# Softmax denominators by 32x32 turns and sums on VectorE, with their inverses spread by way of DRAM

## The chip, the cores and the metric

The kernel runs on one core of a Trainium2 chip. The metric is device time in microseconds (us) of one execution. The core's engines are named as in the profile: PE is TensorE (PEld its weight loads), DVE is VectorE, ACT is ScalarE, POOL is GpSimd, and SP is the engine whose queue issues nearly all DMAs.

## The reference

One transformer block with windowless attention and relative positions, followed by a Fourier layer. Only the attention matters here. All data are float32.

```python
B, H, W, C = 1, 48, 48, 768            # 2304 tokens, 12 heads of 64
xn = layernorm(x, ln1_g, ln1_b)
q, k, v = xn @ qkv_w + qkv_b           # each (12, 2304, 64)
attn = einsum('bqc,bkc->bqk', q * 64**-0.5, k)
attn = attn + rel_h[:, :, :, :, None] + rel_w[:, :, :, None, :]
attn = softmax(attn, axis=-1)
out = einsum('bqk,bkc->bqc', attn, v)  # divided by the softmax's denominators
x = x + out @ proj_w + proj_b
x = x + mlp(layernorm(x))              # GELU, 4 * 768 wide
x = x + spectral_layer(x)              # FFT, two complex block-diagonal layers, inverse FFT
```

## The kernel before

The program goes through normalisation with q, k and v (to about 420 us of the profiled execution), attention (to about 1460), the output projection, the MLP with row transforms, and the spectral layer. The change lies in attention.

Attention is cut into 36 blocks: six head pairs `pr` of two heads each, and in each pair six groups `c` of G = 384 queries. Scores are kept transposed, with 128 keys on partitions and queries along the free dimension, so a softmax denominator is a sum over partitions. A block runs in two phases on TensorE:

- Scores. For each of NT = 18 key tiles `kt`, `content` (L560) multiplies keys by queries and `position` (L569) adds the two relative terms by way of a selection matrix, both into a PSUM tile `sp` with three buffers. ScalarE takes the exponential of each (L579) into `exps`. No maximum is subtracted. VectorE adds the exponentials up two key tiles at a time (`pairs`, L659, eight sums per block) and folds the result into `acc` (L663), a tile of 128 partitions by 2 heads by 384 queries. Only the sum over the partitions is then left.
- Products. In six steps of three key tiles, `products` (L592) multiplies values by exponentials into the PSUM tile `op`. Between the steps, small jobs from the table `between` are put in: `relative` (L292) prepares the row terms of a block three ahead, `columns` (L268) the column terms of the next pair. Both write a PSUM bank `small` (there is one), which ScalarE copies twice (L236, L237) and VectorE splits into two parts (`row_lo`, `col_lo`, L238). After `relative`, SP issues 24 DMAs that repeat the row and column terms into `terms` (L305, L309).

Before step 5, `denominators` multiplies `acc` by a matrix of ones (L603), which sums over the partitions and leaves each head's denominators on all of its 64 partitions. ScalarE copies them to `rden` and also sums them into `sums` (L608). After the last step, `finish` copies `op` to `ot` (L617, ScalarE), adds the value bias times the denominator (L618, VectorE), inverts the denominators (L621), multiplies (L623), adds the inverses into `inverse` (L624, GpSimd) and writes the result to DRAM (`oT`, L625, SP). In the blocks c = 2 and 3, `in_columns` (L584) then copies three slices each of the next pair's queries into `by_column` on ScalarE.

`sums` and `inverse` serve a test after attention: if a denominator or an inverse is not below 1e15, an attention with subtracted maxima runs instead. With the given inputs it doesn't.

The order of the work is fixed in two ways. These lines put the queues of TensorE, SP and ScalarE into the order in which the program states their instructions:

```python
with tc.manual_schedule(engines={mybir.EngineType.PE, mybir.EngineType.SP}):
    ...
                with tc.manual_schedule(engines={mybir.EngineType.Activation}):
```

For VectorE and GpSimd a scheduler chooses the order when the program is laid out, from when it expects operands to be ready and, among ready instructions, by their place in the program. [...]

Of the kernel before, what the change touches and what calls it, by code (L numbers as in the profile page):

```python
# [10 lines left out]
F32 = mybir.dt.float32  # L11
# [3 lines left out]
ALU = mybir.AluOpType  # L15
# [31 lines left out]
def block_then_afno(  # L47
# [42 lines left out]
    def col(i):  # L90
        return vec[:, i : i + 1]
# [9 lines left out]
    k_d = [dram.tile([P, T], F32, name=f"k_d{i}") for i in range(NC)]  # L101
    v_d = dram.tile([T, C], F32, name="v_d")
    oT = dram.tile([C, T], F32, name="oT")

    big1 = ctx.enter_context(tc.tile_pool(name="big1", bufs=1))
    main = big1.tile([P, NT * C], F32, name="main")
# [84 lines left out]

    with ExitStack() as flag_scope:
        flag_pool = flag_scope.enter_context(tc.tile_pool(name="flag", bufs=1))
        sums = flag_pool.tile([P, NC * (T // G)], F32, name="sums")
        inverse = flag_pool.tile([P, G], F32, name="inverse")
        nc.vector.memset(inverse, 0.0)


# [5 lines left out]
        with ExitStack() as att:  # L204
# [18 lines left out]
            def small_bank():  # L223
                banks.append(banks.pop(0))
                return banks[-1]
# [317 lines left out]
            with tc.manual_schedule(engines={mybir.EngineType.PE, mybir.EngineType.SP}):  # L543
                with ExitStack() as qkv:
                    queries_keys_values(qkv)

                psum = att.enter_context(tc.tile_pool(name="ps_att", bufs=1, space=PSUM))
                small_banks(psum, 1)
                kv_b = att.enter_context(tc.tile_pool(name="att_kv_b", bufs=1))
                o_pool = att.enter_context(tc.tile_pool(name="att_o", bufs=2))  # L550

                by_column = o_pool.tile([P, HW, HW], F32, name="by_column", bufs=1)
                kv = [None, kv_b]
                exps = main.rearrange("p (n j q) -> p n j q", n=NT, j=2)

                def content(pr, c, kt, sp, first):
                    qT, kT = heads[pr][:2]
                    for j in range(2):
                        at = slice(64 * j, 64 * j + 64)
                        nc.tensor.matmul(  # L560
                            sp[:, j, :G], kT[at, ts(kt, P)], qT[at, ts(c, G)],
                            start=first, stop=not first,
                        )

                def position(pr, c, kt, sp, first):
                    a, b = divmod(kt, 3)
                    for j in range(2):
                        at = slice(64 * j, 64 * j + 64)
                        nc.tensor.matmul(  # L569
                            sp[:, j, :G], select[at, a % 2], ready[pr, c][at, a // 2, b],  # L570
                            start=first, stop=not first,
                        )

                def scores(pr, c, kt, p):

                    sp = psum.tile([P, 2, 512], F32, name="sp", bufs=3)
                    for n, part in enumerate((content, position)):
                        part(pr, c, kt, sp, n == 0)
                    nc.scalar.activation(p, sp[:, :, :G], AF.Exp, scale=HD**-0.5)  # L579

                def in_columns(pr, i):

                    q = heads[pr][0].rearrange("p (c b h w) -> p b w c h", c=6, b=3, h=8)
                    nc.scalar.copy(  # L584
                        by_column[:, ts(i, 8)].rearrange("p w (c h) -> p w c h", c=6),
                        q[:, i // 2, ds(8 * (i % 2), 8)],
                    )

                def products(op, v, kts):
                    for kt in kts:  # L590
                        for j in range(2):
                            nc.tensor.matmul(  # L592
                                op[ts(j, 64)], v[:, kt, ts(j, 64)], exps[:, kt, j, :],
                                start=(kt == 0), stop=(kt == NT - 1),
                            )

                made = {}

                def denominators(pr, c, acc):

                    den = small_bank()
                    for j in range(2):
                        nc.tensor.matmul(  # L603
                            den[ts(j, 64)], ones[:, 0:64], acc[:, j, :], start=True, stop=True
                        )
                    at = pr * (T // G) + c
                    rden = o_pool.tile([P, G], F32, name="rden", bufs=1)
                    nc.scalar.activation(  # L608
                        rden, den, AF.Identity, accum_out=sums[:, at : at + 1]
                    )  # L610
                    made[pr, c] = rden

                def finish(pr, c, op):

                    rden = made.pop((pr, c))
                    ot = o_pool.tile([P, G], F32, name="ot")
                    nc.scalar.copy(ot, op)  # L617
                    nc.vector.scalar_tensor_tensor(  # L618
                        ot, rden, col(V_VB + pr), ot, ALU.mult, ALU.add
                    )  # L620
                    nc.vector.reciprocal(rden, rden)  # L621
                    o = o_pool.tile([P, G], F32, name="o")
                    nc.vector.tensor_tensor(by_rows(o), by_blocks(ot), by_blocks(rden), ALU.mult)  # L623
                    nc.gpsimd.tensor_tensor(inverse, inverse, rden, ALU.add)  # L624
                    nc.sync.dma_start(out=oT[ts(pr, P), ts(c, G)], in_=o)  # L625

                def between(pr, c, acc):

                    last = pr == NC - 1
                    work = {5: [partial(denominators, pr, c, acc)]}  # L630
                    if c < 3:
                        work[0] = [partial(relative, pr, c + 3)]
                    elif not last and c < 5:
                        for n in range(3):
                            work[n] = [partial(columns, pr + 1, 3 * (c - 3) + n)]
                        if c == 4:
                            work[3] = [partial(relative, pr + 1, 0)]
                    elif not last:
                        work[0] = [partial(relative, pr + 1, 1)]
                        work[2] = [partial(relative, pr + 1, 2)]  # L640
                    return work

                with tc.manual_schedule(engines={mybir.EngineType.Activation}):
                    for pr in range(NC):
                        for c in range(T // G):
                            if c == 1 and pr < NC - 1:
                                fetch(pr + 1, kv[(pr + 1) % 2])
                            if c == 2 and pr < NC - 1:
                                fetch_values(pr + 1)
                            if c == 4 and pr == NC - 1:  # L650
                                nc.sync.dma_start(
                                    out=pw, in_=proj_w.rearrange("(c p) f -> p c f", p=P)
                                )
                            pairs = o_pool.tile([P, 2, 2, G], F32, name="pairs", bufs=1)
                            for kt in range(NT):
                                scores(pr, c, kt, exps[:, kt])
                                if kt > 2 and kt % 2:
                                    so_far = exps[:, ds(0, 2)] if kt == 3 else pairs
                                    nc.vector.tensor_tensor(  # L659
                                        pairs, so_far, exps[:, ds(kt - 1, 2)], ALU.add  # L660
                                    )
                            acc = o_pool.tile([P, 2, G], F32, name="acc")
                            nc.vector.tensor_tensor(acc, pairs[:, 0], pairs[:, 1], ALU.add)  # L663
                            op = psum.tile([P, G], F32, name="op")
                            work = between(pr, c, acc)
                            for i in range(6):
                                for what in work.get(i, ()):
                                    what()
                                products(op, heads[pr][2], range(3 * i, 3 * i + 3))
                            finish(pr, c, op)  # L670
                            if c in (2, 3) and pr < NC - 1:
                                for i in range(3):
                                    in_columns(pr + 1, 3 * (c - 2) + i)

        ln2 = flag_scope.enter_context(tc.tile_pool(name="ln2", bufs=4))
        for i in range(4):
# [847 lines left out]
```

## Time and profile before

| | us |
|---|---|
| median of 3 runs (lowest to highest) | 2895.36 (2893.09 to 2896.4) |
| the profiled execution's own time | 2893.09 |
| span of its profile | 2891.3 |
| PE busy in the span | 2833.2 (98%) |
| DVE busy | 1754.9 (61%) |
| ACT busy | 932.2 (32%) |
| POOL busy | 616.9 (21%) |

The granted clock of TensorE was 0.998 over the span. A busy time counts a group's instructions from start to modelled end with overlaps merged; two TensorE instructions that overlap in the array are each listed with their whole duration. A float32 matmul appears as two instructions. "Idle before, releaser" names the instruction whose end ended the idle time. The profile's times run from the span's start.

### The profile page before, as it was taken

Reading aid. Unit: us, or ns where it says so; the run is one execution under the profiler, and the core shown is the slowest. Engines: PE = TensorE matmul, PEld = TensorE weight load, DVE = VectorE, ACT = ScalarE, POOL = GpSimd, SP = SyncE. Lnnn points to the kernel's source line nnn. Section 1 sums busy time; section 2 is a strip of 40 time slices with the busy share of each in tenths; the row PEclk is TensorE's granted clock in tenths of the full one; section 3 lists DMA queues with packets and bytes.
Section 4 is the critical chain, followed back from the end, with each engine's and each line's share of the span. In section 5 each row is a group of like instructions: output and inputs, shape, how many; then the busy total and the mean of one; then the engine's idle time right before and its main releaser. Section 6 shows DMA issues by size and latency. Waiting matters only on the chain. (4 is left out here: it accounts for less than half of the span.)

```text
span 2891.3 us, 41229 instructions
## 1 busy us (share of the span) xinstructions
PE 2833.2 (98%) x15949; PEld 1724.3 (60%) x15949; DVE 1754.9 (61%) x2412; ACT 932.2 (32%) x1538; POOL 616.9 (21%) x589
## 2 busy tenths in 40 slices
PE   8999999999999999999999999999999999999998
PEld 5555655655555555555555555555555555556887
DVE  5243236767676776767633666675666666666666
ACT  1011125757566665665500210112110211012332
POOL 2303010000000000000043223333323322321433
PEclk9999999999999999999999999999999999999999
DMA  4323276262552716435252111212211211113254
GB/s 153 130 96 107 104 161 127 37 130 58 87 125 42 145 31 107 105 59 87 59 178 77 50 53 57 66 44 88 66 55 55 99 55 55 55 56 114 63 158 143
DMA packets 216572, 255.59 MB, mean 88 GB/s; under 512 B 22220, under 2 KB 197036, under 8 KB 214832
## 3 DMA queue, kind: packets, MB, share of 16 engines
q1 hardware_dynamic: 213928, 251.03, 34.1%
q8 instruction: 128, 2.10, 0.3%
q10 hardware_dynamic: 2440, 1.84, 0.2%
q14 instruction: 76, 0.62, 0.1%
HBM read 136.88 MB, written 52.20 MB: 65 GB/s over the span
## 5 line engine op out<-in xcount | busy, mean ns | idle before, releaser
L579 ACT ACTIVATE main<-sp 128x768 f32<-128x768 f32 x648 | 512.6, 811 | 28.2 <-PE sp L569 14.0
L659 DVE TENSOR_TENSOR pairs<-pairs,main 128x1536 f32<-128x1536 f32 x252 | 443.1, 1758 | 27.1 <-DVE pairs L659 0.9
L569 PE MATMUL sp<-terms,select 64*128 64x384 f32 x1296 | 412.3, 629 | 0.0
L1057 DVE TENSOR_TENSOR main<-o,main 128x384 f32<-128x384 f32 x540 | 299.3, 556 | 39.6 <-PE o L1055 1.3
L995 PE MATMUL h<-shared,w 128*128 128x384 f32 x864 | 296.6, 486 | 0.8 <-issue 0.8
L560 PE MATMUL sp<-shared 64*128 64x384 f32 x1296 | 265.9, 486 | 8.0 <-ACT main L579 5.9
L560 PE MATMUL sp<-qT,kT 64*128 64x384 f32 x1296 | 264.4, 485 | 3.5 <-ACT main L579 3.5
L624 POOL TENSOR_TENSOR inverse<-inverse,rden 128x384 f32<-128x384 f32 x36 | 49.0, 1361 | 989.7 <-DVE rden L621 940.3
L449 PE MATMUL m<-main 128*128 128x384 f32 x756 | 246.0, 487 | 3.3 <-DVE main L176 2.7
L995 PEld LDWEIGHTS h<-shared,w 128*128 128x128 f32 x864 | 164.1, 190 | 116.6 <-issue 3.2
L995 PE MATMUL h<-shared,w1s 128*128 128x384 f32 x648 | 226.6, 486 | 0.0
L592 PE MATMUL op<-main,shared 128*64 128x384 f32 x1296 | 218.7, 487 | 0.0
L592 PE MATMUL op<-main,v 128*64 128x384 f32 x1296 | 217.7, 487 | 0.0
L1001 ACT ACTIVATE hT<-c,vec 128x384 f32<-128x384 f32 x108 | 66.4, 615 | 465.9 <-DVE c L1007 465.8
L449 PEld LDWEIGHTS m<-main 128*128 128x128 f32 x756 | 142.9, 190 | 104.0 <-issue 4.8
L1007 DVE TENSOR_TENSOR c<-h,u 128x384 f32<-128x384 f32 x108 | 60.2, 557 | 212.3 <-PE h L995 212.3
L1055 PE MATMUL o<-w,hT 128*128 128x384 f32 x432 | 175.5, 488 | 3.1 <-DVE mv L122 2.0
L1055 PE MATMUL o<-w2s,hs 128*128 128x384 f32 x432 | 175.0, 487 | 3.0 <-DVE hs L159 3.0
L569 PEld LDWEIGHTS sp<-terms,select 64*128 64x128 f32 x1296 | 125.4, 186 | 83.6
L995 PEld LDWEIGHTS h<-shared,w1s 128*128 128x128 f32 x648 | 123.1, 190 | 85.9
L618 DVE SCALAR_TENSOR_TENSOR ot<-rden,vec,ot 128x384 f32<-128x384 f32 x36 | 23.8, 660 | 244.2 <-ACT ot L617 244.2
L158 POOL TENSOR_TENSOR w1s<-w 128x384 f32<-128x384 f32 x36 | 36.7, 1020 | 602.2 <-PE o L1055 332.2
(161 smaller groups left out, 4065.7 us busy)
## 6 DMA issues: line engine op xcount, KB each, us to landing
w<-in_mlp_w_dram SPq DMA_DIRECT2D x72, 768.0 KB
terms<-col_parts SPq DMA_DIRECT2D x432, 72.0 KB
terms<-row_hi SPq DMA_DIRECT2D x216, 72.0 KB
terms<-row_lo SPq DMA_DIRECT2D x216, 72.0 KB
main<-in_qkv_w_dram SPq DMA_DIRECT2D x36, 384.0 KB
z<-zt SPq DMA_DIRECT2D x48, 192.0 KB
x<-in_x_blocks_dram SPq DMA_DIRECT2D x18, 384.0 KB
k_d<-o SPq DMA_DIRECT2D x36, 192.0 KB
```

The costliest lines, as they stand in the source:

```text
L449: nc.tensor.matmul(bank, a[:, c, :], b[:, c, :], start=(first and c == 0), stop=(c == 2), skip_group_check=not first,)
L560: nc.tensor.matmul(sp[:, j, :G], kT[at, ts(kt, P)], qT[at, ts(c, G)], start=first, stop=not first,)
L569: nc.tensor.matmul(sp[:, j, :G], select[at, a % 2], ready[pr, c][at, a // 2, b], start=first, stop=not first,)
L579: nc.scalar.activation(p, sp[:, :, :G], AF.Exp, scale=HD**-0.5)
L592: nc.tensor.matmul(op[ts(j, 64)], v[:, kt, ts(j, 64)], exps[:, kt, j, :], start=(kt == 0), stop=(kt == NT - 1),)
L624: nc.gpsimd.tensor_tensor(inverse, inverse, rden, ALU.add)
L659: nc.vector.tensor_tensor(pairs, so_far, exps[:, ds(kt - 1, 2)], ALU.add)
L995: nc.tensor.matmul(bank[i], a[:, c, :], b[:, c, :], start=(start and c == 0), stop=(c == 2), skip_group_check=not start,)
L1001: nc.scalar.activation(h[:, i, ts(k, G)], src, AF.Gelu, bias=col(V_B1 + 2 * n + i))
L1007: nc.vector.tensor_tensor(t, src, other, ALU.add)
L1055: nc.tensor.matmul(bank[k], a, b, start=start, stop=True, skip_group_check=not start)
L1057: nc.vector.tensor_tensor(dst, bank[k], dst, ALU.add)
```

## The change

In `denominators`, VectorE now turns `acc` in 32x32 squares (`turned`) and sums over each square's free dimension, which leaves 24 columns of partial sums (`part`, of 48 columns, the rest zero). In the new `inverses`, which stands before step 4 instead of 5, one product of `part` with `gather` (a 128x32 matrix that adds up the four groups of 32 partitions) gives all 768 denominators on 24 partitions of 32. VectorE inverts them there and adds them into `sums`; GpSimd adds the inverses; SP writes them to the DRAM tile `den_d`. In `finish`, two DMAs read them back, each repeated over 64 partitions (`spread`); VectorE multiplies `ot` by it, and the value bias is added on GpSimd afterwards. The ScalarE copy of the denominators, VectorE's scaled bias and its 128x384 reciprocal are gone. The `in_columns` copies move from behind `finish` to places between the steps of `products`.

```diff
--- before.py
+++ after.py
@@ -101,6 +101,7 @@
     k_d = [dram.tile([P, T], F32, name=f"k_d{i}") for i in range(NC)]
     v_d = dram.tile([T, C], F32, name="v_d")
     oT = dram.tile([C, T], F32, name="oT")
+    den_d = dram.tile([NC * (T // G), 2 * G], F32, name="den_d")
 
     big1 = ctx.enter_context(tc.tile_pool(name="big1", bufs=1))
     main = big1.tile([P, NT * C], F32, name="main")
@@ -191,8 +192,9 @@
 
     with ExitStack() as flag_scope:
         flag_pool = flag_scope.enter_context(tc.tile_pool(name="flag", bufs=1))
-        sums = flag_pool.tile([P, NC * (T // G)], F32, name="sums")
-        inverse = flag_pool.tile([P, G], F32, name="inverse")
+        sums = flag_pool.tile([P, 32], F32, name="sums")
+        inverse = flag_pool.tile([P, 32], F32, name="inverse")
+        nc.vector.memset(sums, 0.0)
         nc.vector.memset(inverse, 0.0)
 
 
@@ -594,40 +596,56 @@
                                 start=(kt == 0), stop=(kt == NT - 1),
                             )
 
-                made = {}
+                ND = 2 * G // 32
+                gather = o_pool.tile([P, 32], F32, name="gather", bufs=1)
+                nc.vector.tensor_reduce(
+                    gather, ident.rearrange("p (g a) -> p a g", a=32), AX.X, ALU.add
+                )
+                parts = [o_pool.tile([P, 48], F32, name=f"part{i}", bufs=1) for i in range(2)]
+                for part in parts:
+                    nc.vector.memset(part, 0.0)
 
                 def denominators(pr, c, acc):
 
+                    at = pr * (T // G) + c
+                    turned = o_pool.tile([P, 2 * G], F32, name="turned", bufs=1)
+                    nc.vector.transpose(turned, acc.rearrange("p j q -> p (j q)"))
+                    part = parts[at % 2]
+                    nc.vector.tensor_reduce(
+                        part[:, :ND], turned.rearrange("p (b i) -> p b i", i=32), AX.X, ALU.add
+                    )
+                    return part
+
+                def inverses(pr, c, part):
+
+                    at = pr * (T // G) + c
                     den = small_bank()
+                    nc.tensor.matmul(den[:48, :32], part, gather, start=True, stop=True)
+                    rden = o_pool.tile([ND, 32], F32, name="rden")
+                    nc.vector.reciprocal(rden, den[:ND, :32])
+                    nc.vector.tensor_tensor(sums[:ND], sums[:ND], den[:ND, :32], ALU.add)
+                    nc.gpsimd.tensor_tensor(inverse[:ND], inverse[:ND], rden, ALU.add)
+                    nc.sync.dma_start(out=den_d[at].rearrange("(n i) -> n i", i=32), in_=rden)
+
+                def finish(pr, c, op):
+
+                    at = pr * (T // G) + c
+                    spread = o_pool.tile([P, G], F32, name="spread")
                     for j in range(2):
-                        nc.tensor.matmul(
-                            den[ts(j, 64)], ones[:, 0:64], acc[:, j, :], start=True, stop=True
+                        nc.sync.dma_start(
+                            out=spread[ts(j, 64)], in_=den_d[at, ts(j, G)].partition_broadcast(64)
                         )
-                    at = pr * (T // G) + c
-                    rden = o_pool.tile([P, G], F32, name="rden", bufs=1)
-                    nc.scalar.activation(
-                        rden, den, AF.Identity, accum_out=sums[:, at : at + 1]
-                    )
-                    made[pr, c] = rden
-
-                def finish(pr, c, op):
-
-                    rden = made.pop((pr, c))
                     ot = o_pool.tile([P, G], F32, name="ot")
                     nc.scalar.copy(ot, op)
-                    nc.vector.scalar_tensor_tensor(
-                        ot, rden, col(V_VB + pr), ot, ALU.mult, ALU.add
-                    )
-                    nc.vector.reciprocal(rden, rden)
                     o = o_pool.tile([P, G], F32, name="o")
-                    nc.vector.tensor_tensor(by_rows(o), by_blocks(ot), by_blocks(rden), ALU.mult)
-                    nc.gpsimd.tensor_tensor(inverse, inverse, rden, ALU.add)
+                    nc.vector.tensor_tensor(by_rows(o), by_blocks(ot), by_blocks(spread), ALU.mult)
+                    nc.gpsimd.tensor_scalar(o, o, col(V_VB + pr), None, ALU.add)
                     nc.sync.dma_start(out=oT[ts(pr, P), ts(c, G)], in_=o)
 
                 def between(pr, c, acc):
 
                     last = pr == NC - 1
-                    work = {5: [partial(denominators, pr, c, acc)]}
+                    work = {4: [partial(inverses, pr, c, denominators(pr, c, acc))]}
                     if c < 3:
                         work[0] = [partial(relative, pr, c + 3)]
                     elif not last and c < 5:
@@ -638,6 +656,12 @@
                     elif not last:
                         work[0] = [partial(relative, pr + 1, 1)]
                         work[2] = [partial(relative, pr + 1, 2)]
+                    if not last and c in (2, 3):
+                        for n in range(3):
+                            i = 3 * (c - 2) + n
+                            work.setdefault(n + (1, 3)[c - 2], []).append(
+                                partial(in_columns, pr + 1, i)
+                            )
                     return work
 
                 with tc.manual_schedule(engines={mybir.EngineType.Activation}):
@@ -668,9 +692,6 @@
                                     what()
                                 products(op, heads[pr][2], range(3 * i, 3 * i + 3))
                             finish(pr, c, op)
-                            if c in (2, 3) and pr < NC - 1:
-                                for i in range(3):
-                                    in_columns(pr + 1, 3 * (c - 2) + i)
 
         ln2 = flag_scope.enter_context(tc.tile_pool(name="ln2", bufs=4))
         for i in range(4):
```

## The prediction

> **What bounds the kernel now.** I read the busy shares first, then the attention stage alone (420 to 1460 us) as a stretch and by TensorE's groups, then the timeline of a few blocks.
>
> ```profile
> PE 2833.2 (98%) x15949; PEld 1724.3 (60%) x15949; DVE 1754.9 (61%) x2412; ACT 932.2 (32%) x1538; POOL 616.9 (21%) x589
> ```
>
> The stretch table (busy time of PE, weight loads, DVE, ACT, POOL; clock; DMA share; GB/s) and the group of the denominators (busy, mean ns):
>
> ```profile
> 420.00:1460.00 1040.00, 1031.03 (x8622) 598.08 (x8622) 728.28 (x493) 635.23 (x911) 49.15 (x36) 1.00 0.45 88
> ```
>
> ```profile
> L603 PE MATMUL small<-acc,ones 128*64 128x384 f32 x144 | 29.3, 486 | 0.0
> ```
>
> TensorE works 1031 of 1040 us there at full clock; VectorE works 70%. So work taken from TensorE shortens the stage, unless another engine becomes late. Busy times overlap in a pipelined array, so I take an instruction's price from the distance between starts:
>
> ```profile
> 705.20 0.81 PE L603 MATMUL small<-acc,ones 128*64 128x384 f32 x4
> ...
> 705.85 2.10 PE L592 MATMUL op<-main,v 128*64 128x384 f32 x12
> ```
>
> The four denominator matmuls hold the array 0.65 us per block, 36 times. The second loss follows `finish` of c = 2 and 3 (columns: start, duration, engine, line):
>
> ```profile
> 883.60 2.36 ACT L584 COPY by_column<-qT 128x384 f32<-128x384 f32 x3
> ...
> 886.72 0.92 PE L560 MATMUL sp<-shared 64*128 64x384 f32 x4 [0.89 <-ACT main L579]
> ```
>
> The three copies stand ahead of the next block's exponentials on ScalarE; TensorE fills three score buffers and stops. Scores start every 0.82 us (884.03, 884.85), so the fourth was due at 885.67 and comes 1.05 us late. The chain of waits has it 11 times.
>
> VectorE's margin, in block pr = 2, c = 0 (scores begin at E = 768.14):
>
> ```profile
> 769.49 2.55 DVE L621 RECIPROCAL rden<-rden 128x384 f32<-128x384 f32 x1
> 772.07 0.56 DVE L623 TENSOR_TENSOR o<-ot,rden 128x384 f32<-128x384 f32 x1
> 772.63 2.48 DVE L659 TENSOR_TENSOR pairs<-main 128x1536 f32<-128x1536 f32 x1
> 775.21 12.93 DVE L659 TENSOR_TENSOR pairs<-pairs,main 128x1536 f32<-128x1536 f32 x7
> 788.25 0.96 DVE L663 TENSOR_TENSOR acc<-pairs 128x768 f32<-128x768 f32 x1
> 789.13 0.55 DVE L238 TENSOR_TENSOR row_lo<-shared,row_hi 128x384 fp32r<-128x384 f32 x1
> ...
> 793.55 0.81 PE L603 MATMUL small<-acc,ones 128*64 128x384 f32 x4
> ```
>
> `acc` is ready at 789.2 and wanted at 793.55: 4.3 us to spare. The seven pair sums run back to back, so VectorE is behind the exponentials here and whatever is put among them delays `acc`.
>
> The DMA queue of `relative`, c = 1:
>
> ```profile
> 813.04 0.59 SPq L305 DMA_DIRECT2D terms<-row_hi  x1
> ...
> 828.62 0.60 SPq L309 DMA_DIRECT2D terms<-col_parts  x1
> 829.32 0.53 SPq L625 DMA_DIRECT2D oT<-o  x1
> ```
>
> 24 issues take 16.2 us; block c = 1 ends at about 824.3, so the queue is 5 us behind, harmlessly.
>
> **What the skill says.** *Vector Engine (DVE) Microarchitecture Reference*, 3.8: the 32x32 transpose passes one element per cycle and lane. *VectorE: DVE Perf Modes*, "Rules for kernel authors": tensor_reduce runs at the plain rate. The trace has no transpose; its plain 768-element sum (`acc`) takes 0.96, and its 384-element reduction 0.55. *GPSIMD Engine Reference*, Specifications: GpSimd shares SBUF interfaces with two-input VectorE work. The trace agrees: the first pair sum takes 2.48 beside the `inverse` sum (POOL, 1.36), else 1.76. *DMA: Bandwidth & Descriptors*, "Anatomy of one DMA": some 2.0 us fixed, given for the software path; nothing here waits on a comparable transfer, so it is unconfirmed.
>
> **The change, part by part.**
>
> *TensorE.* Removed: 36 x 0.65 = 23.4 us. Added: one product with 48 weight columns and 32 moving columns, as two instructions. Nearest rows: the lone `line` transpose (128 moving columns) starts at 1476.37 and the next matmul at 1476.47, 0.10 us; 32 small products of L268 hold the array 0.71. I take 0.10, with 0.05 and 0.35 as bounds (weights badly hidden). Net 36 x 0.55 = **-19.8 us** (-10.8 to -21.6).
>
> *Copies.* The six `in_columns` of each of five head pairs go between products, where ScalarE idles for 5 us and more. Ten stalls of 1.05 go: **-10.5 us**. If the cover failed, 3 x 0.85 us would stand ahead of `ot` instead, no worse than now. The first needs qT of the next pair, fetched a block earlier; see the queue below.
>
> *ScalarE.* `rden` and its accumulator read (0.49 + 0.19) go; they lie in idle time: nothing.
>
> *VectorE.* Per block: out 0.66 + 2.55; in: turn and sum at 0.96 each (bounds 0.85, and 1.75 at half rate), two sums on 24x32 at about 0.2. It gains time, but turn and sum come **between** `acc` and TensorE, and the product is wanted one step (1.94 us) earlier, at E + 23.4 instead of E + 25.4. Without the reciprocal ahead, pair sums start when four exponentials are done, E + 4.3; they end 1.76 + 7 x 1.85 + 0.09 later, E + 19.1; then `acc`, turn, sum at 0.96 + 0.09: E + 22.2. In hand: 1.1 us. Against it: `o` multiplied amid the pair sums (0.65), GpSimd's bias addition beside one (up to 0.72), `row_lo` slipped in (0.55): at worst 24.1, a wait of 0.8. Blocks c = 3, 4 have two or three more column products ahead (0.71 each), against as many 0.85 us `col_lo`. I take 0.2 us on average: **+7 us** (0 to 29). Behind the waiting product TensorE queues the last two steps of products and the next scores.
>
> *SP queue.* Per block: the write of `rden`, waiting for the product (E - 3.5) and all term transfers; two spreads, waiting for that write to land; `oT` behind both, waiting for `o` and GpSimd. Issues: 3 x 0.6. With 2.2 us per landing, spreads land at E + 2 (c = 3), +10 (c = 1, 2) and past +20 (c = 5, 48 issues). Each pair adds some 13 us of landings (6 x 2.2), 25 of waits for `o` (6 x 4, an estimate) and 11 of issues to about 100 of issues (6 x 24 x 0.64 and the `oT`, fetches) in 171 (6 blocks of 28.5): the queue falls behind at c = 4 to 1 and recovers by c = 3. Terms are wanted three blocks later, and qT, now issued some 26 us into a block and wanted 46 us in, has its 8 us. Nothing on the end's path, if `o` stands late enough in VectorE's order.
>
> *GpSimd.* The addition on 24x32 replaces 1.36 us; the bias pass (128x384) takes about 1 (96x192 takes 0.70). Idle engine: nothing beyond the sharing counted.
>
> Sum: -19.8 - 10.5 + 7 = **-23 us**. The profiled execution took 2893.09 (span 2891.3), 2.3 below the median of the runs; from it 2870, from the median 2872. I give 2871.
>
> **Rivals.**
>
> *R1, slower: `o` waits in VectorE's queue.* VectorE's order is set ahead by the scheduler, from expected landings. If `o` stands before the pair sums and the spread lands at E + 10, these start 6 us late, the part comes at E + 28.5 and TensorE waits 5; a wait moves E toward the queue's clock, so about half lasts. It decides from a landing about 6 us after E on. Price: 18 blocks of c = 0 to 2 x 2.5 = 45 us, c = 4 and 5 some 10 each: 2870 + 45 + 100 = about 3010; for c = 0 to 2 alone 2915. Against it: in the later pairs `row_lo` of c = 0 to 2 stands behind `acc`, though `row_hi` was done 3 us before: the order expects SP's backlog to be long.
>
> *R2: the part is late.* At half rate, turn and sum add 1.6 us to every block: waits of about 1.4 x 36 = 50, so 2893 - 30 + 50 = 2913; at 0.8 late it cancels the gain. For: the thin 1.1 us. Against: the plain rate on page and rows.
>
> *R3: the new product costs what the old did* (weights not hidden, its wait breaking the stream): -10.5 + 7, 2890, no change to speak of.
>
> **Chances.** As forecast 0.62; R1 0.13; R2 0.17 (a third of it near zero); R3 0.08. Faster by over 0.2% (6 us, about what a measurement of this kernel can tell) 0.63, same 0.09, slower 0.28. The forecast's own range is 2861 to 2885; for eight in ten it must reach R2 and the milder R1: 2861 to 2918.
>
> **What would show it.** L603 gone, a product of well under 0.2 us per block in its place; no wait of scores on ScalarE after c = 2, 3; L584 inside the products; a TensorE wait for VectorE at the product of about 0.2 us; `o` amid the pair sums or after the part, never with idle time ahead of it (VectorE idle on a DMA of 5 us would be R1); turn and sum near 0.96 (1.7 would be R2). I am wrong if the wait at the product averages over 0.8 us.

## The result and the profile after

| | us |
|---|---|
| before, median of 6 runs | 2896.45 (2893.09 to 2898.01) |
| after, median of 6 runs | 3037.6 (3033.9 to 3039.93) |
| ratio after to before | 1.0488, interval 1.0474 to 1.0501 |
| profiled execution of after, own time; span | 3038.3; 3036.2 |

The change made the kernel slower by 141 us; the forecast of 2871 lay 25 below before. First the busy share of TensorE on the page of after:

```profile
PE 2835.9 (93%) x15877; PEld 1744.3 (57%) x15877; DVE 1697.1 (56%) x2488; ACT 919.7 (30%) x1466; POOL 632.6 (21%) x625
```

TensorE had 98% before. It has no more to do than then (15877 instructions against 15949); it stands still. The waits of TensorE in after (waiting line, releaser, us in total, times, longest) say where:

```profile
PE small L270 <- ACT col_parts L239: 121.1, 5, 26.8
PE sp L562 <- ACT main L581: 21.3, 4, 5.6
...
PE small L623 <- DVE part L614: 9.6, 1, 9.6
```

L270 is the product of `columns`. Five stops, one in each head pair that has a next one, take 121 us. Only the last of the three, which comes once, is at an instruction that the change has put in.

The rewritten parts themselves did as forecast. A product of an undisturbed block, in TensorE's timeline of after (start, duration):

```profile
839.24 0.19 PE L623 MATMUL small<-gather,part 128*48 128x32 f32 x1
839.25 0.54 PE L594 MATMUL op<-main,shared 128*64 128x384 f32 x1
```

The next product starts 0.01 us behind it. The groups of the turn and the sum (busy, mean ns):

```profile
L612 DVE STREAM_TRANSPOSE turned<-acc 128x768 f32<-128x768 f32 x36 | 35.2, 978 | 1.2
L614 DVE TENSOR_REDUCE part<-turned 128x24 f32<-128x768 f32 x36 | 34.3, 952 | 1.1
```

Both stand near the 0.96 of the plain 768-element sum. Where nothing stops, a block is shorter. The end of a block shows in ScalarE's timeline as `ot`:

```profile
843.43 0.48 ACT L639 COPY ot<-op 128x384 f32<-128x384 f32 x1 [10.53 <-PE op L594]
870.97 0.48 ACT L639 COPY ot<-op 128x384 f32<-128x384 f32 x1 [10.87 <-PE op L594]
```

The distance is 27.54 us; before, the copies `ot` at the two ends of such a block start at 768.25 and 796.34, 28.09 apart. 0.55 us a block is gained, and then lost several times over.

**Following one stop back.** I took the stop in the third head pair. ScalarE's timeline, then TensorE's:

```profile
902.88 2.29 ACT L586 COPY by_column<-qT 128x384 f32<-128x384 f32 x3 [15.24 <-DMA qT<-q_d]
...
921.33 0.48 ACT L238 COPY shared<-small 128x384 f32<-128x384 f32 x1
948.93 0.80 ACT L239 CAST col_parts<-small 128x384 fp32r<-128x384 f32 x1 [27.12 <-DMA terms<-row_lo]
```

```profile
921.11 2.12 PE L594 MATMUL op<-main,shared 128*64 128x384 f32 x12
949.78 1.52 PE L270 MATMUL small<-by_column,relT 128*48 128x48 f32 x32 [26.55 <-ACT col_parts L239]
```

The first column product (c = 3) is copied out of `small` at 921.33. The second copy of it goes into `col_parts`, and `col_parts` has one buffer: the transfers into `terms` that c = 2 asked for still have to read it. ScalarE waits 27 us for them (the view names a transfer of `row_lo`; which one it was is worked out below). `small` is one bank, so the second column product can't start, and TensorE stands behind it. At 902.88 it is the same with the copies of `in_columns`: qT of the next pair is late, and the exponentials of the next block stand behind these copies (the 21.3 us at L562).

Why were the transfers late? SP's timeline, with its term transfers left out:

```profile
846.68 0.55 SPq L628 DMA_DIRECT2D den_d<-rden  x1
849.56 1.14 SPq L635 DMA_DIRECT2D spread<-den_d  x2
869.33 0.33 SPq L643 DMA_DIRECT2D oT<-o  x1
869.77 0.64 SPq L307 DMA_DIRECT2D terms<-row_hi  x1
...
897.24 0.43 SPq L256 DMA_DIRECT2D qT<-q_d  x1
...
929.29 0.33 SPq L643 DMA_DIRECT2D oT<-o  x1
...
944.02 0.59 SPq L311 DMA_DIRECT2D terms<-col_parts  x1
...
947.85 0.59 SPq L311 DMA_DIRECT2D terms<-col_parts  x1
```

Between 850.7 and 869.33 SP issues nothing: it stands at the store `oT`, which waits for GpSimd's bias addition, which waits for `o`. The 24 term transfers behind it start when it goes, without a further wait. So the queue reaches the transfers of c = 2 only after 929.29. `col_parts` has two halves. The last transfer that reads the half which ScalarE overwrites is issued at 944.02; its semaphore is full at 948.83, and the copy starts at 948.93. (The semaphore serves other transfers too, hence the other name in the view.) The half that VectorE overwrites is read last by the transfer of 947.85, and VectorE starts on it at 952.51.

The longest of these stands, the one shown, comes of VectorE's order:

```profile
864.64 0.95 DVE L614 TENSOR_REDUCE part<-turned 128x24 f32<-128x768 f32 x1
865.51 0.55 DVE L240 TENSOR_TENSOR row_lo<-shared,row_hi 128x384 fp32r<-128x384 f32 x1
867.11 0.34 DVE L625 RECIPROCAL rden<-small 24x32 f32<-24x32 f32 x1 [1.05 <-issue]
867.39 0.12 DVE L626 TENSOR_TENSOR sums<-sums,small 24x32 f32<-24x32 f32 x1
867.43 0.53 DVE L641 TENSOR_TENSOR o<-ot,spread 128x384 f32<-128x384 f32 x1
```

This `o` is not of the block that ended at 843.43 (c = 0 of this pair) but of the one before it, which ended at 815.9; its spread was issued at 849.56. From the second pair to the fifth, the scheduler has put the `o` of c = 5, 0 and 1 behind `part` of the second block on, and that of c = 2 and 4 behind `part` of the next; only that of c = 3 goes ahead of it. Here `o` comes 51.5 us after its copy of `op` and 18 after the first half of its spread was issued. The waits of SP in sum:

```profile
SPq L643 <- POOL o L642: 342.6, 36, 18.6
...
SPq L635 <- DMA den_d<-rden: 81.9, 36, 8.8
```

9.5 us per block at the store (342.6 / 36), 2.3 at the landing of the inverses. The stands at the store differ: from the end of the second spread's issue to the store they are 7.4, 5.8, 8.0, 5.8, 11.5 and 18.2 us for c = 0 to 5 of the third pair. The `o` of c = 3 follows its copy by 3.8 us, so some 5.8 are what landing, product and bias take in any case, and what is over that, some 22 us a pair, comes for the greater part from the late `o` of c = 4 and 5.

### The profile page after: what moved, and what is told of

Same layout as the page of the kernel before. It is cut to its first block, busy times and chain, and to the rows that moved or that the text cites. A ratio compares the mean times of both kernels' runs of the same rounds, so it can differ in the third digit from the quotient of the medians.

```text
span 3036.2 us, 41272 instructions
## 1 busy us (share of the span) xinstructions
PE 2835.9 (93%) x15877; PEld 1744.3 (57%) x15877; DVE 1697.1 (56%) x2488; ACT 919.7 (30%) x1466; POOL 632.6 (21%) x625
## 5 line engine op out<-in xcount | busy, mean ns | idle before, releaser
L581 ACT ACTIVATE main<-sp 128x768 f32<-128x768 f32 x648 | 519.3, 813 | 37.2 <-PE sp L571 27.0
L571 PE MATMUL sp<-terms,select 64*128 64x384 f32 x1296 | 418.6, 638 | 0.0
L562 PE MATMUL sp<-shared 64*128 64x384 f32 x1296 | 270.7, 494 | 12.5 <-ACT main L581 10.3
L562 PE MATMUL sp<-qT,kT 64*128 64x384 f32 x1296 | 269.6, 493 | 11.1 <-ACT main L581 11.1
L627 POOL TENSOR_TENSOR inverse<-inverse,rden 24x32 f32<-24x32 f32 x36 | 14.9, 413 | 929.3 <-DVE sums L626 889.0
L683 DVE TENSOR_TENSOR pairs<-main 128x1536 f32<-128x1536 f32 x36 | 63.3, 1758 | 254.3 <-ACT main L581 254.2
```

The source lines that it names most:

```text
L562: nc.tensor.matmul(sp[:, j, :G], kT[at, ts(kt, P)], qT[at, ts(c, G)], start=first, stop=not first,)
L571: nc.tensor.matmul(sp[:, j, :G], select[at, a % 2], ready[pr, c][at, a // 2, b], start=first, stop=not first,)
L683: nc.vector.tensor_tensor(pairs, so_far, exps[:, ds(kt - 1, 2)], ALU.add)
```

## The experiments

My theory, A: the store `oT` holds SP's queue, the terms come late, and the overwriting of `col_parts` turns that into stops of TensorE. The rivals, with the letters of the expectations: the landings and issues of the round trip over DRAM are more than the queue can carry (B); its transfers compete for the DMA engines (C); the moved copies, which wait for a late qT, do it (D); the turns, the sums or the moved product do it (E); `o` waits in VectorE's queue amid the pair sums (R1 of the prediction). The first four ran beside 15 runs of before (median 2896.05), the last four beside 7 (2896.86).

**e1_store_later: the same store, one block later on SP's queue.** Against after:

```diff
                     nc.gpsimd.tensor_scalar(o, o, col(V_VB + pr), None, ALU.add)
-                    nc.sync.dma_start(out=oT[ts(pr, P), ts(c, G)], in_=o)
+                    if stores:
+                        store()
+                    stores.append((pr, c, o))
```

(`store` issues the oldest entry; one more call stands at the end.)

> The changed kernel, but the store of a block's result (oT) is issued one block later on SP, behind that block's two spreads, and nothing else is edited. Theory A (SP's queue stands still at the store, because o is multiplied only after the next block's partial sums; the terms, the fetch of qT and v then come late, and ScalarE and TensorE stop at c = 2 and 3): the SP waits at the store, 342.6 us in the changed kernel, fall under 60; TensorE's waits for col_parts (121 us) and for the late exponentials (21 us) go; about 2893 - 30 = 2866 to 2875 us. Theory B (the round trip itself, its landing waits of 82 us and some 60 us of issues, is what the queue can't carry): still over 2980 us. Theory C (the transfers compete for the DMA engines): still over 2980 us.

Measured: 2879.71 (2875.11 to 2886.27), ratio to before 0.9946 (0.9928 to 0.9965). 158 us came back from a change of place of 36 stores. It is 5 us above the top of what A gave, and SP still waits at the store for 86.4 us where under 60 were expected. The waits of SP (L635 is the store here), and TensorE's at `columns`:

```profile
SPq L635 <- POOL o L649: 86.4, 13, 24.0
```

```profile
PE small L270 <- ACT col_parts L239: 9.9, 4, 3.3
```

One block later is not enough where `o` stands two blocks late; hence e7 below.

**e2_copies_undone: `in_columns` back behind `finish`.**

```diff
-                    if not last and c in (2, 3):
-                        for n in range(3):
...
                             finish(pr, c, op)
+                            if c in (2, 3) and pr < NC - 1:
+                                for i in range(3):
+                                    in_columns(pr + 1, 3 * (c - 2) + i)
```

> The changed kernel with the six by_column copies per pair put back behind finish of c = 2 and 3. Theory A: the wait for qT (some 14 us of ScalarE per pair at c = 2, 5 of TensorE) is nearly gone since the copies come some 12 us later, but the stop at col_parts stays, and ten stalls of 1.05 us come back: 3020 to 3045 us. Rival D (the moved copies, waiting for qT ahead of the exponentials, are the cause): under 2940 us.

Measured: 3045.18 (3044.97 to 3049.1), ratio 1.0518 (1.05 to 1.0535), with 121.2 us of TensorE waiting for `col_parts` in five stops as in after. The moved copies are not the cause; D falls.

**e3_copies_alone: the same move of the copies, in the kernel before.**

> The kernel before with only the by_column copies moved between the steps of products. All theories: the ten waits of scores on ScalarE go, 10.5 us, 2886 us. If qT came late for them even here: not under 2893.

Measured: 2883.62 (2882.97 to 2884.59), ratio 0.9957 (0.994 to 0.9974): 12.4 us gained, where 10.5 were expected. No wait of scores for exponentials is left in the waits of TensorE.

**e4_trip_added: a round trip over DRAM added to the kernel before.** Per block one write of the same size and two spreads, on SP, about where after has them. The data written are ones, and no result reads them: only work is added.

```diff
                     made[pr, c] = rden
+                    nc.sync.dma_start(
+                        out=den_d[at].rearrange("(n i) -> n i", i=32), in_=ones[0:24, 0:32]
+                    )
...
+                    spread = o_pool.tile([P, G], F32, name="spread")
+                    for j in range(2):
+                        nc.sync.dma_start(
+                            out=spread[ts(j, 64)], in_=den_d[at, ts(j, G)].partition_broadcast(64)
+                        )
```

> The kernel before with the round trip alone added on SP: per block a write of 24x32 numbers (ones, read by nobody who matters) to DRAM behind the term transfers, and two spreads of it over 64 partitions, which nothing on the engines waits for; the result's path is as before. Theory A: the queue has room for it, 2890 to 2905 us. Theory B: 2980 us or more. Theory C: 2980 us or more.

Measured: 2894.79 in 12 runs (2892.28 to 2899.2), ratio 0.9999 (0.999 to 1.0007). The waits of SP show that the trip is really waited for, and where it finds room. SP's wait at the store in the kernel before, then the same and the wait for the landing in this one:

```profile
SPq L625 <- DVE o L623: 203.6, 8, 30.2
```

```profile
SPq L635 <- DVE o L633: 124.6, 8, 22.2
SPq L623 <- DMA den_d<-ones: 71.6, 36, 8.5
```

So SP stood at the store before the change as well, and it cost nothing: five of the eight stands, 29 to 30 us each, are at c = 3, and the transfers behind them are not ready until some 20 us later still. That is SP's spare time, and the trip takes a part of it. 72 us of landings and 108 more issues on SP cost nothing. B and C fall: the trip by itself is not the loss.

**e5_o_early: `o` pinned ahead of the next block's first pair sum**, in after. This was to be a clean R1.

```diff
+                                    if kt == 3 and scaled:
+                                        tc.add_manual_dep(
+                                            pair.ins, scaled.pop(0).ins.name,
...
+                                            reason="scaled first",
+                                        )
```

> The changed kernel with o pinned in VectorE's order ahead of the next block's first pair sum (an order of issue only). The store then comes as soon as the spread has landed, so SP stands at it for a few us per block and the waits at col_parts go; VectorE stands instead, up to 6 us where one term transfer is ahead of the spread and over 15 us where two are. This is the prediction's R1 at full strength: TensorE waits at the product for the part, 80 to 150 us in all: 2940 to 3010 us. If VectorE's order didn't matter to SP: 3030 to 3040, as the changed kernel.

Measured: 3220.55 (3215.8 to 3222.96), ratio 1.1116 (1.1097 to 1.1134), far above what was expected. The waits of VectorE in it, and SP's at the store:

```profile
DVE row_lo L240 <- ACT row_hi L239: 414.0, 35, 22.3
...
DVE o L644 <- DMA spread<-den_d: 90.3, 16, 10.6
```

```profile
SPq L649 <- POOL o L648: 282.2, 36, 19.5
```

The pin made the scheduler lay out more than `o` differently. It also put `row_lo` ahead of `o` and of the pair sums, so VectorE stood until the scores were through; the pair sums, and with them `part`, came late in 27 blocks (301.6 us of TensorE at L623). The wait that R1 is about is 90 of the 504 us here. The run doesn't price R1, and I leave that price open. It does say what such a pin can do. SP, too, stands longer at the store than the few microseconds that were expected, and yet no stop at `col_parts` is left: a pair takes some 235 us here. The total of SP's waits alone doesn't make the loss; what counts is whether the transfers are through in time.

**e6_before_store_late: the delay alone, in the kernel before.** e4's trip, the old denominators, inverse and copies, and `o` pinned behind the next block's `acc`, or behind that of the second block on for c = 5, 0 and 1, nearly as after has it (there, that of c = 3 goes early); `rden` and `ot` get three buffers for that.

```diff
-                    nc.vector.tensor_tensor(by_rows(o), by_blocks(ot), by_blocks(rden), ALU.mult)
+                    scaled = nc.vector.tensor_tensor(
+                        by_rows(o), by_blocks(ot), by_blocks(rden), ALU.mult
+                    )
+                    waiting.append((int(c in (5, 0, 1)), scaled))
...
+                                tc.add_manual_dep(
+                                    scaled.ins, folded.ins.name,
...
+                                    reason="late",
+                                )
```

> The kernel before, its ones product, reciprocal and copies kept, with two edits: the round trip of e4_trip_added, and o pinned late in VectorE's order, as it stands in the changed kernel: behind the next block's acc, or behind the one after it for c = 5, 0 and 1. Theory A (late o, store in order on SP): the loss appears without any turn, sum or small product: TensorE waits at col_parts for some 24 us in each of five pairs, about 3000 us, at least 2960. Theory E (the loss belongs to the turns, sums or the moved product): 2890 to 2910 us.

Measured: 3021.17 (3019.22 to 3023.82), ratio 1.0427 (1.041 to 1.0444). The waits of TensorE, then of SP:

```profile
PE small L269 <- ACT col_parts L238: 114.3, 5, 23.9
```

```profile
SPq L639 <- DVE o L634: 383.7, 30, 40.9
```

The same five stops and 126 us more than e4 (3021.17 - 2894.79), without a turn, a sum over squares or the new product; E falls. With the trip there, a late `o` whose store stands ahead of the terms on SP's queue is enough. No run has the late `o` without the trip.

**e7_store_two_later: e1, with the store two blocks later** (`o` in four buffers, `ot` and `spread` in three; two calls at the end). Against e1:

```diff
-                    if stores:
+                    if len(stores) > 1:
                         store()
```

> As e1_store_later, but the store is issued two blocks later (o in four buffers, ot and spread in three), since o stands up to two blocks late in VectorE's order. Theory A: SP's waits at the store (86 us left in e1) are nearly gone, with them the four stops at col_parts (9.9 us) and the slower clock behind them: 2862 to 2872 us, 8 to 18 below e1. If those waits cost nothing: as e1, 2880.

Measured: 2865.08 (2864.48 to 2865.44), ratio 0.989 (0.9873 to 0.9906). SP waits 25.0 us at the store, three times, and of the stops at `col_parts` 0.6 us is left, once.

**e8_store_gpsimd: the store on another queue.** The one word in which it differs from after:

```diff
-                    nc.sync.dma_start(out=oT[ts(pr, P), ts(c, G)], in_=o)
+                    nc.gpsimd.dma_start(out=oT[ts(pr, P), ts(c, G)], in_=o)
```

> The changed kernel with the store issued by GpSimd instead of SP, behind the bias addition that it waits for anyway; nothing else is edited, o stays as late as it was. Theory A: nobody stands behind that wait any more, so 2862 to 2880 us. Theory B or C (the round trip or the transfers themselves): over 2980 us.

Measured: 2864.03 (2862.43 to 2865.72), ratio 0.9889 (0.9872 to 0.9905): level with e7, 32.8 us under before and 173.6 under after. GpSimd waits for `o` itself, one instruction earlier in the same chain, so nothing new stands behind the store. TensorE works 1019.4 of the 1020 us from 420 to 1440. One block of it, TensorE's timeline, then VectorE's `part`:

```profile
812.92 0.92 PE L562 MATMUL sp<-shared 64*128 64x384 f32 x4
...
836.39 0.19 PE L623 MATMUL small<-gather,part 128*48 128x32 f32 x1
...
840.46 0.92 PE L562 MATMUL sp<-shared 64*128 64x384 f32 x4
```

```profile
834.25 0.95 DVE L614 TENSOR_REDUCE part<-turned 128x24 f32<-128x768 f32 x1
```

The block is 27.54 us long. `part` is ready at 835.20, 1.2 us before its product; `o` stands as late in VectorE's order as in after, and it harms nobody.

**The account.** The spans of after and e8 differ by 175.6 us (3036.2 - 2860.6). TensorE's three waits of after, which e8 has not, make 152.0 (121.1 + 21.3 + 9.6). With the same 15877 instructions it is also busy for 24.1 us longer (2835.9 against 2811.8 on e8's page). That is the clock: summed over TensorE's busy time, the records of the granted clock give 29.4 us lost at half speed in after and 6.1 in e8, 23.3 apart. A window on the stop in after (busy PE, weight loads, DVE, ACT, POOL; granted clock; DMA share; GB/s) reads:

```profile
926.00:950.00 24.00, 0.22 (x6) 0.22 (x8) 1.89 (x3) 0.80 (x1) 1.24 (x1) 0.51 0.83 131
```

So the products behind a stop begin at half speed: the 32 of L270 at 949.78 took 1.52 us, those at 920.36, ahead of it, 0.93. Waits and clock make 152.0 + 24.1 = 176.1. *TensorE: Matmul & The Clock Gate* of the Trainium skill, "What's actually happening", says that the array falls to half its clock after an idle window of about 3.4 us; this case agrees: TensorE stood still from 923.23, the record of half clock begins at 926.57, and the window shown has 0.51.

One way to take the last link away, a second buffer for `col_parts`, wasn't tried.

## Why the prediction was wrong, step by step

**TensorE, -19.8: right.** 0.55 us per block was forecast, and blocks of 27.54 against 28.09 show 0.55. e8 less the copies gives 20.4 (32.8 - 12.4). R3 is out: the next product starts 0.01 us after the new one.

**Copies, -10.5: right**, 12.4 measured alone (e3), with an uncertainty of some 5. In after they waited for qT 15.24 us in the place shown, so their cover, qT's margin of 8 us, failed with the queue, not by itself.

**VectorE, +7 for a late part: too much.** In the block shown `part` was ready at E + 22.3 (835.20 - 812.92) and its product ran at E + 23.5; E + 22.2 and E + 23.4 were forecast. The average wait of 0.2 us didn't come: e8 has no wait of TensorE at the product. R2 is out with it, at 0.98 and 0.95 for turn and sum. The sharing of SBUF that I had charged against the margin went the other way: the first pair sum, 2.27 us on average before, takes 1.76 in after, as GpSimd's wide `inverse` sum no longer runs beside it.

**SP queue, put at nothing: the step that failed.** Clearing that queue alone took 173.6 us off after (e8). Three terms of the step were wrong.

- The waits for `o`. "25 of waits for `o` (6 x 4, an estimate)" came to 57 per pair (6 x 9.5). Even where `o` is early the stand took 5.8 and not 4; the late `o` of c = 4 and 5 added most of the rest. The landings, 13 forecast (6 x 2.2), were 14 (6 x 2.3; the skill's *DMA: Bandwidth & Descriptors*, "Anatomy of one DMA", which I could not confirm before, has some 2.0 for the software path, and SP's is near it). So, with the forecast's 100 and 11 for issues, a pair needs an estimated 100 + 11 + 14 + 57 = 182 us of SP, and an undisturbed pair takes 169.6 (e8, from one copy of `op` at 785.50 to the same copy of the next pair at 955.14). I had 149 in 171. The queue doesn't recover by c = 3.
- The deadline. "Terms are wanted three blocks later" counts from the reader of `terms`. The first who needs these transfers done is `col_parts`, which c = 3 overwrites: one block after c = 2 asks for them. That one has a single buffer, and I looked at none of the buffers on the source side of the transfers.
- The condition had the wrong sign. "Nothing on the end's path, if `o` stands late enough in VectorE's order": I asked only who stands behind `o` on VectorE, and not who waits for its result. Where `o` comes latest after its spread, at c = 5, SP stands longest at the store (18.2 us). The late place of `o`, which I counted as evidence against R1, made the loss together with the place of the store on SP's queue.

**R1** ended on the right side, by another way. VectorE waits in `o` for a spread 52.1 us in seven places of after; five are at c = 3, with no wait of TensorE behind them; one, in the last pair, stands amid the pair sums, as R1 had it, and reaches TensorE with the 9.6 us at L623 of the 152. R1's price is not what the 141 are, so that the kernel came out near its "about 3010" is chance (its terms 2870 + 45 + 100 make 3015).

By its own sum, with the part's wait at 0 and the queue kept clear, the change is -19.8 - 10.5 = -30.3; e7 and e8 measure -31.8 and -32.8.

## What to carry to other kernels

A store that waits for a result holds everything behind it on the queue that issues it, as SP's did here. So when its producer is moved, ask who is queued behind the store, and put it behind them or on the producer's own queue. A transfer has two deadlines: its reader's, and the next overwriting of its source; with one source buffer the second is often the nearer. And putting an instruction "late enough" in one queue is safe only if nobody in another queue waits for it at a fixed place.

## What the runs showed of the hardware

- The stores issued from GpSimd took 0.59 us each to issue and landed after 2.2 to 7.4 us (median 2.9). That SP's order, not the DMA engines, was the scarce thing shows in e8: the same bytes, and 173.6 us less than after.
- The bias addition on GpSimd took 1.24 us alone and 2.52 beside `col_lo` on VectorE (863.32 in e8); I had given it about 1.
- A stop of TensorE costs more than itself, and the surplus doesn't grow with the stop. By the records of the granted clock in after, the five stops of 16.8 to 26.8 us each cost a further 1.4 to 2.6 us of busy time at half clock, the four of 5.1 to 5.6 us 1.6 to 2.9, and the one of 9.6 us 2.9. The half clock was recorded from 3.3 to 5.1 us after TensorE had begun to stand still in these ten.
